# Two transformer layers on one core: the planner's passes, layer 0's queries through DRAM, and the first loads on two queues

## The chip, the cores and the metric

The kernel runs on one core of a Trainium2 chip. The metric is the device time of one execution in microseconds (us), given as the median over runs. A core has five engines with instruction streams of their own: TensorE (PE, with its weight loads shown apart as PEld), VectorE (DVE), ScalarE (ACT), GpSimd (POOL) and SyncE (SP, which issues most DMAs here). They meet through semaphores.

## The reference

Two layers over four batches of 256 rows of 512 numbers, all in float32, with a context of 1601 rows for each batch. Cut to what is computed:

```python
# layer 0: latent cross attention (16 heads, latent width 32) and an int4 FFN
C_q = ln(x) @ Wq_d                       # 512 -> 64
C_kv = ctx @ Wkv_d                       # 512 -> 32, shared by all heads
q0 = (C_q @ W_qk).reshape(b, n, 16, 32)
attn = softmax(q0 @ C_kv.T / sqrt(32))
x = x + attn @ (C_kv @ Wv_u)             # per head
x = x + ln(x) @ dequantize(weight_q, scale, zero_point).T + bias
# layer 1: grouped-query attention (16 heads, 4 KV heads, width 96), keys from [ctx, ln(x)]
q, k, v = ln(x) @ Wq.T, concat(ctx, ln(x)) @ Wk.T, concat(ctx, ln(x)) @ Wv.T
x = x + softmax(q @ k.T / sqrt(96)) @ v @ Wo.T
# layer 1: FFN with gated low-rank experts
H = ln(x) @ W.T + b;  z = ln(x) @ A
gate = f(H[:, 1::2, :8] / max|H|, (z[:, 1::2] @ LiMEs.T) / max|.|)  # softmax, soft top 2, over all batches
x = x + H + ((z * (gate @ LiMEs)) @ Bmat) * scaling
```

The two maxima in the gate go over all four batches, so the last part of the program waits for the last batch.

## The kernel before

**Stages.** A string, LINE (L1533 on), gives the order of the attention heads: 16 of layer 0 for batch 0, then, three times, a mix of layer 1's 16 heads of one batch with layer 0's 16 heads of the next, and then 16 heads of layer 1 for batch 3. Between a batch's two kinds of heads stand the layer-0 FFN (tiles f0) and layer 1's queries, keys and values.

**Order.** All work between the first loads and the gate is a set of tasks with hand-written costs, buffers and dependencies. `Plan.order` (L63 to L134) places them in one pass: of all tasks that are ready it takes the one with the earliest start, then the lowest `prio` (the place of its head in LINE plus an offset such as AT_SCORES). The result is the program order of every engine, the DMA queue on SP included; each engine then works strictly in that order. A task that needs a buffer can't be placed until the ring of its tag has a free one: 8 buffers for scores in SBUF ("S"), two for scores in PSUM ("s"), two for the stage tag "p" (normalised rows, parts of w0, and the query rows of layer 1 on their way to DRAM), two for layer 0's queries ("q0"), one for the transposed context ("ctxT", 3.3 MB).

**One head.** PE makes transposed scores in tiles of 32 rows, four side by side (L1306 in layer 0, L1382 in layer 1). ACT copies them to SBUF (L1162), DVE takes maxima over the key tiles (L1180 to L1188), PE turns the result (L1211), DVE reduces it (L1215), PE spreads it (L1224), DVE copies it (mB, L1232) and subtracts it from the scores (L1241), ACT takes the exponential (L1250), and PE multiplies with the values (L1333 in layer 0 with tiles of 64 columns, L1407 in layer 1 with full tiles). Between the heads PE makes K (L795) and V (L737) of the next layer-1 stage from the context.

**Layer 0's queries** (L643 to L669). For a pair of heads two matmuls of 64x128 by 64x256 (L649) give the queries of the pair, each copied four times over the partitions, since the score tiles use four row groups. The weights w_qk are loaded four times for that (L209 on, eight DMAs). ACT copies 512 columns to the q0 buffer (L658). Layer 1's queries go another way: PE, ACT into a stage of tag "p", a DMA to DRAM (q_rows), and DMAs back into the four row groups.

**FFN weights of layer 0** (make_w0, L477 on). Loads of the integers, zero points and scales, then DVE and POOL work, into w0T (L510 is POOL's).

**Start.** All loads are on SP: x, wq_d, w_qk, wkv_d, context, values' weights, keys' weights. POOL makes the identity matrix.

**End.** end_layer1 (L1526) normalises, calls l1_gate (z, g and d by PE, L1017 to L1081), and the FFN (tiles f, L532). After the plan come the gate's steps by DVE, POOL and ACT (L1659 to L1709), its transpose (wts_tp, L1716), the mix (L1721) and the output (L1740).

Of the kernel before, what the change touches and what calls it, by code (L numbers as in the profile page):

```python
# [62 lines left out]
class Plan:  # L63

    LAG = {"PE": 0.2, "ACT": 0.1, "DVE": 0.07, "POOL": 0.15, "SP": 0.05, "INIT": 0.0}
# [4 lines left out]
    def task(self, eng, us, what, deps=(), prio=0.0, new=(), uses=(), lag=0.0):  # L70

        t = Task(eng, us, what, [d for d in deps if d is not None], prio, new, len(self.tasks))
        t.lag = lag
        for b in (*new, *uses):
            b.users.append(t)
        self.tasks.append(t)
        return t

    def order(self, busy):

        free, ready, rings, done = {}, {}, {}, []
        for t in self.tasks:
            t.wait = len(t.deps)
            for d in t.deps:
                d.next.append(t)
            free.setdefault(t.eng, busy.get(t.eng, 0.0))
            ready.setdefault(t.eng, [])
            if not t.wait:
                t.at = 0.0
                ready[t.eng].append(t)  # L90

        def buffers(t):
            at, more = 0.0, {}
            for b in t.new:
                ring = rings.setdefault(b.tag, [])
                n = len(ring) + more.get(b.tag, 0)
                more[b.tag] = more.get(b.tag, 0) + 1
                if n >= b.bufs:
                    for u in ring[n - b.bufs].users:
                        if u.end is None:  # L100
                            return None
                        at = max(at, u.end + self.LAG[u.eng])
            return at

        while len(done) < len(self.tasks):
            best = None
            for eng, tasks in ready.items():
                for t in tasks:
                    at = buffers(t) if t.new else 0.0
                    if at is None:  # L110
                        continue
                    key = (max(free[eng], t.at, at), t.prio, t.key)
                    if best is None or key < best[0]:
                        best = (key, t)
            if best is None:
                stuck = [t for tasks in ready.values() for t in tasks]
                raise ValueError(f"no task can start: {[(t.eng, [b.tag for b in t.new], t.prio) for t in stuck]}")
            t = best[1]
            ready[t.eng].remove(t)
            t.start = best[0][0]  # L120
            free[t.eng] = t.start + t.us
            t.end = t.start + t.us + t.lag
            for b in t.new:
                rings[b.tag].append(b)
            for n in t.next:
                n.wait -= 1
                if not n.wait:
                    n.at = max(
                        d.end + (0.0 if d.eng == n.eng and not d.lag else self.LAG[d.eng])
                        for d in n.deps  # L130
                    )
                    ready[n.eng].append(n)
            done.append(t)
        return done  # L134


@with_exitstack
def xattn_ffn_x2_kernel(
# [47 lines left out]
    ident = const.tile([P, P], F32, name="ident")  # L186
    make_identity(nc, ident)
    neg_half = const.tile([P, NQ], F32, name="neg_half")
    nc.gpsimd.memset(neg_half, -0.5)

    xs = {}
    held = tc.dram_tile([NT * P, D], F32, name="held")

    for t in range(NQ):
        xs[t] = work.tile([P, D], F32, tag="x", bufs=2 * NQ, name=f"x_{t}")
        nc.sync.dma_start(out=xs[t], in_=x[t * P : (t + 1) * P, :])

    def load_ctx(b):  # L200
        t = big.tile([P, NC, S], F32, tag="ctxT", name=f"ctxT_{b}")
        src = ctxT[b].rearrange("(c p) s -> p c s", p=P)
        for a, w in ((0, 512), (512, 512), (1024, S - 1024)):
            nc.sync.dma_start(out=t[:, :, a : a + w], in_=src[:, :, a : a + w])
        return t

    wq_d_sb = const.tile([P, NC, LQ], F32, name="wq_d_sb")
    nc.sync.dma_start(out=wq_d_sb, in_=wq_d.rearrange("(c p) n -> p c n", p=P))


    w_qk_sb = const.tile([P, H0 // 2, 4, L0], F32, name="w_qk_sb")
    for r in range(4):
        for k in range(2):
            nc.sync.dma_start(
                out=w_qk_sb[k * LQ : (k + 1) * LQ, :, r, :],
                in_=w_qk.rearrange("q (k h l) -> k q h l", k=2, l=L0)[k],
            )
    wkv_d_sb = const.tile([P, NC, L0], F32, name="wkv_d_sb")
    nc.sync.dma_start(out=wkv_d_sb, in_=wkv_d.rearrange("(c p) n -> p c n", p=P))
    first_ctx = load_ctx(0)  # L220
# [3 lines left out]
    for r in (0, 64):  # L224
        nc.sync.dma_start(
# [8 lines left out]

    KV_ORDER = [3, 0, 1, 2]
    wvT_sb = const.tile([P, NC, KV * HD], F32, name="wvT_sb")
    for c in range(NC):
        src = wvT[c * P : (c + 1) * P, :]
        nc.sync.dma_start(out=wvT_sb[:, c, :HD], in_=src[:, 3 * HD :])
        nc.sync.dma_start(out=wvT_sb[:, c, HD:], in_=src[:, : 3 * HD])  # L240
# [48 lines left out]
    rsums = tc.dram_tile([B * KV, G * T], F32, name="rsums")  # L289
    q_rows = [  # L290
# [18 lines left out]
    def item(name, steps, evictions, deps, prio, uses=(), new=()):  # L309
# [5 lines left out]
        for us, what in steps:  # L315

            def run(what=what, first=last is None):
# [14 lines left out]
                [*uses] if first else [ps, *uses],  # L332
            )
# [214 lines left out]
    def l0_latents(b, deps, prio):  # L548
# [22 lines left out]
        def keep(ps):  # L571
# [11 lines left out]
            [cT],  # L583
        )
# [30 lines left out]
    def l0_query_latent(b, xnT, deps, prio):  # L615
        cqT = Buf("cqT", 1)


        def step(ps, c):
            for r in range(2):  # L620
                nc.tensor.matmul(
                    ps[r * LQ : (r + 1) * LQ, :T],
                    lhsT=wq_d_sb[:, c, :],
                    rhs=xnT.tile[:, c, :],
                    start=(c == 0),
                    stop=(c == NC - 1),
                )

        def keep(ps):
            nc.scalar.copy(cqT.tile, ps[:, :T])  # L630
# [9 lines left out]
            [(cqT, [P, T])],  # L640
        )

    def l0_query(b, pair, prio):  # L643
        q0, cqT = Buf("q0", 2), st8[b]["cqT"]

        def step(ps, j):
            h = 2 * pair + j
            half = slice(h // 8 * LQ, (h // 8 + 1) * LQ)
            nc.tensor.matmul(  # L649
                ps[:, j * T : (j + 1) * T],  # L650
                lhsT=w_qk_sb[half, h % 8, :, :].rearrange("q r l -> q (r l)"),
                rhs=cqT.tile[half, :],
# [4 lines left out]
        def keep(ps):  # L657
            nc.scalar.copy(q0.tile.rearrange("p j t -> p (j t)"), ps)  # L658

        st8[b]["q0", pair] = q0  # L660
        st8[b]["q0_done", pair] = item(
            f"q0_ps_{b}_{pair}",
            chain(2, mm(T), step),
            [("ACT", cp(512), keep, (), ())],
# [3 lines left out]
            [(q0, [P, 2, T])],  # L668
        )  # L669

# [343 lines left out]
    def l1_gate(b, xnT, deps, w, prio):  # L1014
# [10 lines left out]
        def z_keep(ps):  # L1025
# [11 lines left out]
            [xnT],  # L1037
        )
# [71 lines left out]

    AT_SCORES = -3.0
    AT_COPY = -1.1
    AT_MAX = -1.4
    AT_TURN = -0.9
    AT_SPREAD = -0.5
    AT_SUB0 = -0.6
# [4 lines left out]
    AT_FIN = -2.7  # L1121

    class Head:
# [6 lines left out]
        def schedule(self):  # L1130
# [6 lines left out]
            for groups, units in self.score_units():  # L1137
                for k, (us, what) in enumerate(units):

                    def run(what=what, groups=groups, first=k == 0):  # L1140
# [12 lines left out]
                        self.score_uses() + ([ps[g] for g in groups] if k else []),  # L1153
                    )
# [98 lines left out]
            for g in range(4):  # L1253
                n = self.groups[g] * T
                t = task(
                    "DVE",
                    tt(n),
                    lambda g=g: subtract(g),
                    [t],
                    at + (AT_SUB0 if g < 2 else AT_SUB1),  # L1260
                    uses=[S4[g], mb],
                )
                weighed.append(
                    task(
                        "ACT",
                        cp(n) + 0.05,
                        lambda g=g: weights(g),
                        [t],
                        at + (AT_EXP0 if g < 2 else AT_EXP1),
                        uses=[S4[g]],  # L1270
                    )
                )

            for us, groups, deps, uses, what in self.product_units():
# [6 lines left out]
                    uses=[om, *(S4[g] for g in groups), *uses],  # L1281
                )
            self.finish(om, t)

    class Head0(Head):
        layer, groups, scale = 0, [4, 4, 3, 2], 1.0 / math.sqrt(L0)

# [68 lines left out]
    class Head1(Head):  # L1356
        layer, groups, scale = 1, [4, 4, 4, 3], 1.0 / math.sqrt(HD)

# [119 lines left out]
    def load_context(b, prio):  # L1478
# [5 lines left out]
        st8[b]["cT_done"] = [task("SP", 0.3, run, book.get("x", ()), prio, [cT], lag=kb(3300))]  # L1484

    def start_layer0(b, at, deps):
# [3 lines left out]
        l0_latents(b, st8[b]["cT_done"], at - 5)  # L1490

    def context_work(b, at, deps_v, deps_k):
# [3 lines left out]
        for i in range(3):  # L1496
            ctx_keys(b, i, done + deps_k, at[0] - 4 + 0.2 * i)
        for half in range(2):
            new_values(b, half, at[2 * half] - 4)
            for t in range(NK0):  # L1500
                prio = at[0] - 3 + 1.5 * half + 0.05 * t
                values(b, half, t, cT, ctx_at[t], done + deps_v, prio)
# [59 lines left out]
    st8[0]["cT_done"] = [task("INIT", 0.0, have_ctx, new=[cT], lag=24.0)]  # L1562
    start_layer0(0, 0, ready(7.0))
    w0, w0_done = make_w0(st8[0]["cqT_done"])
    context_work(0, first1[0], ready(33.0), ready(40.0))
    for pair in range(2):
        l0_query(0, pair, -4)
    matrix, matrix_done = w0, w0_done
    for i, (layer, b, h) in enumerate(line):
        where = at[2 * b + layer]  # L1570
        if layer == 0:
            if h % 2 == 0 and h >= 4:
                l0_query(b, h // 2, i - 3)
            elif h == 0 and b:
                for pair in range(2):
                    l0_query(b, pair, i - 4)
# [76 lines left out]
    with tc.manual_schedule(engines=engines):  # L1653
        for t in plan.order({"SP": 40.0}):
# [137 lines left out]
```

## Time and profile before

| | |
|---|---|
| runs | 2025.68, 2028.62, 2031.17 us; median 2028.62 |
| profiled execution | 2031.49 us, span 2029.7 us |
| mean granted clock of TensorE | 0.979 |
| PE, DVE, ACT, POOL busy | 1960.7, 1379.7, 1172.5, 130.6 us |
| first PE instruction, first scores of layer 0 | 13.06, 30.49 us |
| last product of batch 0's layer 0 copied (L1350) | 230.8 us |
| first f0, first layer-1 scores | 252.46, 282.49 us |
| last FFN (f, L532), gate's weights (wts) | 1995.60 to 2005.1, 2007.47 us |
| DMA traffic | 99.01 MB, mean 49 GB/s |

Times inside the execution are microseconds from the start of the span. "Idle before" of a group is the time that its engine stood still before it, with what ended it. A group is named by line, engine, operation, and output and input tiles; a chain gives the work that ended last, in order of time; a window gives busy times of every engine in a stretch.

### The profile page before, as it was taken

The numbers are of one execution on the slowest core, as the hardware profiler recorded it, in microseconds if no ns is written. First come the engines' busy times: TensorE is split into PE (matmuls) and PEld (weight loads), VectorE is DVE, ScalarE is ACT, GpSimd is POOL, SyncE is SP. The second block draws the span as 40 slices with busy tenths as digits, with TensorE's granted clock in tenths as the row PEclk, the third lists the DMA queues.
The fourth block names the chain that finished last, engine by engine and source line by source line (L and its number), as shares of the span: only waits on it lengthen the run. The fifth ranks groups of instructions, "written<-read, shape, count | busy, mean of one in ns | idle before, by whom it ended". The sixth has DMA issues, their size and how long they took to land.

```text
span 2029.7 us, 35881 instructions
## 1 busy us (share of the span) xinstructions
PE 1960.7 (97%) x14873; PEld 1356.1 (67%) x14873; DVE 1379.7 (68%) x2077; ACT 1172.5 (58%) x1776; POOL 130.6 (6%) x171
## 2 busy tenths in 40 slices
PE   6999889999999999999999999999999999999977
PEld 4555667666766686766666777766666668677753
DVE  3876447877787635777778745587888764577653
ACT  3777336666666534666767644466676654465540
POOL 0100200000000100000000200000000010000000
PEclk9999899999999999999999999999999999999996
DMA  6000331110000024121000130512100002211221
GB/s 171 27 1 1 103 104 37 48 40 25 24 17 22 22 63 155 49 53 40 24 17 9 22 83 22 157 48 55 33 16 17 22 21 63 82 50 46 61 59 41
DMA packets 125574, 99.01 MB, mean 49 GB/s; under 512 B 71043, under 2 KB 103971, under 8 KB 125028
## 3 DMA queue, kind: packets, MB, share of 16 engines
q1 hardware_dynamic: 125412, 96.73, 17.2%
q8 instruction: 117, 1.92, 0.4%
q14 instruction: 45, 0.37, 0.1%
HBM read 85.51 MB, written 11.17 MB: 48 GB/s over the span
## 4 chain that ended last, share of the span: by engine, by line
PE 91%; ACT 3%; DVE 2%; DMA 2%; issue 1%; POOL 1%; SPq 0%; ACTq 0%; POOLq 0%; DVEq 0%
PE o L1407 20%; PE s L1382 18%; PE o L1333 10%; PE v_ps L737 8%; PE k_ps_c L795 7%; PE s L1306 7%; PE wo_ps L996 4%; PE q_ps L886 4%; PE f L532 3%; PE o L1211 2%; PE o L1224 2%; PE q_ps L649 1%; PE vu_ps L678 1%; PE k_ps_x L795 1%; ACT S L1250 1%
## 5 line engine op out<-in xcount | busy, mean ns | idle before, releaser
L1162 ACT COPY S<-s 128x1024 f32<-128x1024 f32 (+2 forms) x512 | 449.2, 906 | 374.6 <-PE s L1382 149.3
L1183 DVE TENSOR_TENSOR mx<-mx,S 128x512 f32<-128x512 f32 (+1 forms) x704 | 463.7, 659 | 127.5 <-ACT S L1162 101.1
L1241 DVE TENSOR_TENSOR S<-S,mB 128x1024 f32<-128x1024 f32 (+2 forms) x512 | 532.2, 1097 | 4.4
L1250 ACT ACTIVATE S<-S 128x1024 f32<-128x1024 f32 (+2 forms) x512 | 464.1, 946 | 97.6 <-DVE S L1241 91.1
L1407 PE MATMUL o<-S,v 128*97 128x256 f32 x1920 | 459.7, 383 | 2.1 <-ACT S L1250 2.1
L1407 PEld LDWEIGHTS o<-S,v 128*97 128x97 f32 x1920 | 302.5, 164 | 106.1 <-issue 20.7
L1382 PE MATMUL s<-q,kT_k_ps_c 32*128 32x256 f32 x4320 | 281.0, 386 | 2.2 <-ACT S L1162 1.7
L1382 PEld LDWEIGHTS s<-q,kT_k_ps_c 32*128 32x128 f32 x4320 | 227.7, 186 | 53.3 <-issue 20.8
L1333 PE MATMUL o<-S,ckv 128*64 128x256 f32 x1664 | 229.7, 393 | 4.2 <-ACT S L1250 3.9
L1333 PEld LDWEIGHTS o<-S,ckv 128*64 128x64 f32 x1664 | 115.8, 138 | 103.4 <-ACT S L1250 27.3
L795 PE MATMUL k_ps_c<-ctxT,wk_sb 128*128 128x384 f32 (+1 forms) x480 | 163.6, 462 | 0.2
L737 PE MATMUL v_ps<-wvT_sb,ctxT 128*128 128x192 f32 x832 | 163.2, 337 | 0.0
L1306 PE MATMUL s<-q_q_ps,ckvT 32*128 32x256 f32 x1664 | 150.3, 409 | 3.8 <-ACT S L1162 3.8
L737 PEld LDWEIGHTS v_ps<-wvT_sb,ctxT 128*128 128x128 f32 x832 | 134.8, 192 | 26.1 <-issue 21.7
L1215 DVE TENSOR_REDUCE m<-o 128x2 f32<-128x256 f32 x128 | 54.0, 422 | 130.6 <-PE o L1211 130.6
L1180 DVE TENSOR_TENSOR mx<-S 128x512 f32<-128x512 f32 x128 | 90.8, 709 | 58.5 <-ACT S L1162 58.4
L1306 PEld LDWEIGHTS s<-q_q_ps,ckvT 32*128 32x128 f32 x1664 | 91.8, 185 | 57.1 <-issue 33.0
L795 PEld LDWEIGHTS k_ps_c<-ctxT,wk_sb 128*128 128x128 f32 x480 | 77.3, 189 | 56.3 <-issue 25.5
L996 PE MATMUL wo_ps<-wo,oT 128*128 128x512 f32 x192 | 96.0, 624 | 10.3 <-POOL oT L983 10.3
L886 PE MATMUL q_ps<-xnT_xn_tp_a,wq 128*128 128x256 f32 x384 | 99.9, 392 | 1.4 <-issue 0.8
L805 ACT COPY kT_k_ps_c<-k_ps_c 32x384 f32<-32x384 f32 (+1 forms) x180 | 76.8, 426 | 33.4 <-PE k_ps_c L795 31.2
L1382 PE MATMUL s<-q,kTlast_k_ps_c 32*128 32x256 f32 x1440 | 93.2, 385 | 0.0
(136 smaller groups left out, 1411.6 us busy)
## 6 DMA issues: line engine op xcount, KB each, us to landing
q<-q_rows SPq DMA_DIRECT2D x192, 96.0 KB
wq<-in_wqT SPq DMA_DIRECT2D x48, 192.0 KB
wo<-in_woT SPq DMA_DIRECT2D x16, 576.0 KB
ctxT<-in_ctxT SPq DMA_DIRECT2D x8, 1024.0 KB
q_rows<-p_q_ps SPq DMA_DIRECT2D x48, 128.0 KB
q<-q_rows SPq DMA_DIRECT2D x192, 32.0 KB
ctxT<-in_ctxT SPq DMA_DIRECT2D x4, 1154.0 KB
rb<-rsums SPq DMA_DIRECT2D x16, 288.0 KB
```

The lines of the kernel that those rows point to most:

```text
L737: nc.tensor.matmul(ps[:, : 2 * HD], lhsT=src.tile[:, c, a : a + P], rhs=wvT_sb[:, c, half * 2 * HD : (half + 1) * 2 * HD], start=(c == 0), ...
L795: nc.tensor.matmul(out, lhsT=wk_sb[:, c, i, :], rhs=rhs, start=(c == 0), stop=(c == NC - 1),)
L886: nc.tensor.matmul(ps[:, :T], lhsT=wq.tile[:, c, :], rhs=xnT.tile[:, c, :], start=(c == 0), stop=(c == NC - 1),)
L996: nc.tensor.matmul(ps, lhsT=oT.tile[:, i, q * P : (q + 1) * P], rhs=wo.tile[:, i, :], start=(i == 0), stop=(i == G - 2),)
L1162: nc.scalar.copy(S4[g].tile[:, :n, :], self.scored(ps[g].tile, g))
L1183: nc.vector.tensor_tensor(mx.tile[:, :w, :], mx.tile[:, :w, :], t[:, a : a + w, :], ALU.max)
L1241: nc.vector.tensor_tensor(s[:, :n, :], s[:, :n, :], mb.tile[:, None, :].to_broadcast([P, n, T]), ALU.subtract,)
L1250: nc.scalar.activation(s[:, :n, :], s[:, :n, :], AF.Exp, scale=self.scale)
L1306: nc.tensor.matmul(pss[2 * step + r // 2][:, 2 * (r % 2) + s % 2, :], lhsT=st8[self.b]["ckvT"].tile[part, s, :], rhs=qr[part, self.h % 2, ...
L1333: nc.tensor.matmul(po[64 * par : 64 * par + 64, :], lhsT=s["ckv"].tile[:, t, :, :].rearrange("p o l -> p (o l)"), rhs=self.S[g].tile[:, i, :],
L1382: nc.tensor.matmul(pss[2 * step + r // 2][:, 2 * (r % 2) + slot % 2, :], lhsT=s["kT", self.kv].tile[part, c, slot, :], rhs=s["q1", self.kv ...
L1407: nc.tensor.matmul(po[:VW, :], lhsT=s["v", j // 2].tile[:, t, j % 2, :], rhs=self.S[g].tile[:, i, :], start=(k == 0), stop=(k == NK1 - 1),)
```

## The change

It has three parts.

1. **Planner.** Every task of PE has a form (full, 32 rows, 64 columns, 32 columns, 64 rows). `forward` is the old pass with new constants; a change of form costs SWITCH and adds HOLD to the priority of a task. `backward` goes through the finished order from its end and sets each task's priority to how late it has to end. `order` alternates the two, nine forward passes in all, and keeps the order whose own end is the earliest. The offsets AT_ of the first pass and the due times of the first loads are new too.
2. **Layer 0's queries.** One matmul of 64x128 by 64x256 for four heads, one copy into a stage of tag "p", one DMA to DRAM (q0_rows), and then four DMAs for each pair back into the four row groups. w_qk is loaded once.
3. **Start.** x, wq_d, wkv_d, w_qk and wv_h are loaded by ACT's queue, the context, wv and wk by SP's. The identity is made by DVE from a counted row and a column that is loaded, and POOL's first power is issued at once.

The diff, cut (lines of SELF and OVERLAP are the engines' own gaps; `backward` is left out):

```diff
-    LAG = {"PE": 0.2, "ACT": 0.1, "DVE": 0.07, "POOL": 0.15, "SP": 0.05, "INIT": 0.0}
+
+    LAG = {"PE": 0.22, "ACT": 0.05, "DVE": 0.05, "POOL": 0.1, "SP": 0.05, "INIT": 0.0}
+    SELF = {"ACT": 0.012, "DVE": 0.034}
+    OVERLAP = {"ACT": 0.1, "DVE": 0.084}
+
+
+    SWITCH = 0.2
+    HOLD = 2.0
...
+                    stays = eng != "PE" or t.form == form
+                    key = (
+                        max(free[eng], t.at, at),
+                        t.prio + (0.0 if stays else self.HOLD),
+                        t.key,
+                    )
...
+            if t.eng == "PE" and t.form != form:
+                t.start += self.SWITCH
+            free[t.eng] = t.start + t.us - self.OVERLAP.get(t.eng, 0.0)
...
+    ROUNDS = 8
+
+    def order(self, busy):
+        for t in self.tasks:
+            for d in t.deps:
+                d.next.append(t)
+        best = None
+        for i in range(self.ROUNDS + 1):
+            done = self.forward(busy)
+            end = max(t.end for t in done)
+            if best is None or end < best[0]:
+                best = (end, done)
+            self.backward(done)
+        return best[1]
...
-    ident = const.tile([P, P], F32, name="ident")
-    make_identity(nc, ident)
+
     neg_half = const.tile([P, NQ], F32, name="neg_half")
     nc.gpsimd.memset(neg_half, -0.5)
-
-
-
+    first_power = small.tile([P, NQ], F32, tag="power", bufs=1, name="first_power")
+    nc.gpsimd.memset(first_power, 1.0)
+    nc.gpsimd.tensor_tensor(first_power, first_power, neg_half, ALU.pow)
     xs = {}
-    held = tc.dram_tile([NT * P, D], F32, name="held")
-
     for t in range(NQ):
         xs[t] = work.tile([P, D], F32, tag="x", bufs=2 * NQ, name=f"x_{t}")
-        nc.sync.dma_start(out=xs[t], in_=x[t * P : (t + 1) * P, :])
-
-    def load_ctx(b):
+        nc.scalar.dma_start(out=xs[t], in_=x[t * P : (t + 1) * P, :])
+
+    count = ptile("count")[:, :P]
+    nc.vector.memset(count[:, 0:1], 0.0)
+    for k in (1, 2, 4, 8, 16, 32, 64):
+        nc.vector.tensor_scalar(count[:, k : 2 * k], count[:, :k], float(k), None, ALU.add)
+    number = small.tile([P, 1], F32, tag="number", bufs=1, name="number")
+    nc.scalar.dma_start(out=number, in_=count[0:1, :])
+    ident = const.tile([P, P], F32, name="ident")
+    nc.vector.tensor_scalar(ident, count, number, None, ALU.is_equal)
+    wq_d_sb = const.tile([P, NC, LQ], F32, name="wq_d_sb")
+    nc.scalar.dma_start(out=wq_d_sb, in_=wq_d.rearrange("(c p) n -> p c n", p=P))
+    wkv_d_sb = const.tile([P, NC, L0], F32, name="wkv_d_sb")
+    nc.scalar.dma_start(out=wkv_d_sb, in_=wkv_d.rearrange("(c p) n -> p c n", p=P))
+    w_qk_sb = const.tile([LQ, H0 * L0], F32, name="w_qk_sb")
+    nc.scalar.dma_start(out=w_qk_sb, in_=w_qk)
...
+    first_ctx = load_ctx(0, load_wv)
...
         def step(ps, c):
-            for r in range(2):
-                nc.tensor.matmul(
-                    ps[r * LQ : (r + 1) * LQ, :T],
-                    lhsT=wq_d_sb[:, c, :],
-                    rhs=xnT.tile[:, c, :],
-                    start=(c == 0),
-                    stop=(c == NC - 1),
-                )
+            nc.tensor.matmul(
+                ps[:LQ, :T],
+                lhsT=wq_d_sb[:, c, :],
+                rhs=xnT.tile[:, c, :],
+                start=(c == 0),
+                stop=(c == NC - 1),
+            )
         def keep(ps):
-            nc.scalar.copy(cqT.tile, ps[:, :T])
+            nc.scalar.copy(cqT.tile, ps[:LQ, :T])
         st8[b]["cqT"] = cqT
         st8[b]["cqT_done"] = item(
@@ -637,36 +718,58 @@
             deps,
             prio,
             [xnT],
-            [(cqT, [P, T])],
+            [(cqT, [LQ, T])],
+            "64 columns",
         )
-    def l0_query(b, pair, prio):
-        q0, cqT = Buf("q0", 2), st8[b]["cqT"]
-
-        def step(ps, j):
-            h = 2 * pair + j
-            half = slice(h // 8 * LQ, (h // 8 + 1) * LQ)
+    def l0_query(b, quad, prio):
+
+        stage, cqT, far = Buf("p", 2), st8[b]["cqT"], q0_rows[b * H0 // 4 + quad]
+
+        def step(ps, _):
             nc.tensor.matmul(
-                ps[:, j * T : (j + 1) * T],
-                lhsT=w_qk_sb[half, h % 8, :, :].rearrange("q r l -> q (r l)"),
-                rhs=cqT.tile[half, :],
+                ps[:, :T],
+                lhsT=w_qk_sb[:, quad * P : (quad + 1) * P],
+                rhs=cqT.tile,
                 start=True,
                 stop=True,
             )
         def keep(ps):
-            nc.scalar.copy(q0.tile.rearrange("p j t -> p (j t)"), ps)
-
-        st8[b]["q0", pair] = q0
-        st8[b]["q0_done", pair] = item(
-            f"q0_ps_{b}_{pair}",
-            chain(2, mm(T), step),
-            [("ACT", cp(512), keep, (), ())],
+            nc.scalar.copy(stage.tile[:, :T], ps[:, :T])
+
+        def away():
+            nc.sync.dma_start(out=far, in_=stage.tile[:, :T])
+
+        t = item(
+            f"q0_ps_{b}_{quad}",
+            chain(1, mm(T), step),
+            [("ACT", cp(T), keep, (), ())],
             st8[b]["cqT_done"],
             prio,
             [cqT],
-            [(q0, [P, 2, T])],
+            [(stage, [P, 512])],
+            "64 rows",
         )
+        st8[b]["q0_away", quad] = [task("SP", 0.4, away, t, prio, uses=[stage], lag=2.5)]
+
+    def l0_query_pair(b, pair, prio):
+
+        q0, far = Buf("q0", 2), q0_rows[b * H0 // 4 + pair // 2]
+
+        def load():
+            t = make(q0, [P, 2, T], f"q0_{b}_{pair}")
+            a = pair % 2 * 2 * L0
+            for r in range(4):
+                nc.sync.dma_start(
+                    out=t[r * L0 : (r + 1) * L0],
+                    in_=far[a : a + 2 * L0].rearrange("(j l) t -> l j t", l=L0),
+                )
+
+        st8[b]["q0", pair] = q0
+        st8[b]["q0_done", pair] = [
+            task("SP", 1.6, load, st8[b]["q0_away", pair // 2], prio, [q0], lag=3.0)
+        ]
...
+    AT_COPY = -1.3
...
     def start_layer0(b, at, deps):
 
         xnT, done, _ = layernorm(b, "a0", "xnT", at - 5)
         l0_query_latent(b, xnT, done + deps, at - 5)
-        l0_latents(b, st8[b]["cT_done"], at - 5)
+        for quad in range(H0 // 4):
+            l0_query(b, quad, at - 4.5 + quad)
+        l0_latents(b, st8[b]["cT_done"][-1], at - 5)
...
+    st8[0]["cT_done"] = [[t, *ready(us)] for us in (8.0, 13.0, 16.0)]
+    start_layer0(0, 0, ready(5.0))
     w0, w0_done = make_w0(st8[0]["cqT_done"])
-    context_work(0, first1[0], ready(33.0), ready(40.0))
+    context_work(0, first1[0], ready(11.0), ready(21.0))
     for pair in range(2):
-        l0_query(0, pair, -4)
...
-        for t in plan.order({"SP": 40.0}):
+        for t in plan.order({"SP": 14.0}):
```

## The prediction

> **What bounds the kernel now.** I read the page's busy shares and chain first, then the windows by stage, then the chain of waits at the three places that the change touches: the start, the end of batch 0's layer 0, and the end of the program.
>
> ```profile
> PE 1960.7 (97%) x14873; PEld 1356.1 (67%) x14873; DVE 1379.7 (68%) x2077; ACT 1172.5 (58%) x1776; POOL 130.6 (6%) x171
> PE 91%; ACT 3%; DVE 2%; DMA 2%; issue 1%; POOL 1%; SPq 0%; ACTq 0%; POOLq 0%; DVEq 0%
> ```
>
> TensorE sets the time over most of the span: 91% of the chain is PE. So PE work that is removed counts in full, unless a stage is set by something else. The windows say where (time, then PE, PEld, DVE, ACT, POOL busy, clock):
>
> ```profile
> 50.00:100.00 50.00, 48.07 (x324) 28.62 (x324) 42.77 (x68) 38.69 (x60) 8.75 (x9) 1.00 0.09 28
> 100.00:150.00 50.00, 48.50 (x320) 28.26 (x320) 39.68 (x61) 38.52 (x60) 2.02 (x4) 0.97 0.00 1
> 240.00:290.00 50.00, 40.32 (x300) 30.64 (x303) 13.59 (x29) 9.43 (x25) 8.43 (x9) 0.84 0.36 97
> 1000.00:1200.00 200.00, 199.05 (x1473) 137.11 (x1470) 147.19 (x222) 131.10 (x204) 16.50 (x17) 0.99 0.08 22
> 1960.00:2030.00 70.00, 46.71 (x105) 21.95 (x103) 20.65 (x50) 4.19 (x9) 3.08 (x4) 0.67 0.14 48
> ```
>
> In the first two, batch 0's layer-0 heads, PE is full only because K and V work of layer 1 is mixed in, and VectorE is 80 to 86% busy: a head of layer 0 alone would be VectorE's. The next and the last are stages of waits, with PE at 81 and 67% and a lower clock.
>
> ```profile
> 227.58 0.38 SPq L204
> 229.16 10.12 DMA w_AluOpType.subtract<-in_zeroT
> 239.35 0.74 POOL w0T L510
> 252.46 6.88 PE f L532 x16
> ```
>
> After the last head of layer 0 (230.8) a small load, issued behind the 3.3 MB context load, takes 10.12 us; the FFN of layer 0 waits for it.
>
> ```profile
> 1988.77 3.59 PE z_ps L1017 x8
> 1995.04 0.56 PE d_ps L1081 x2
> 1995.60 6.09 PE f L532 x8
> 2007.47 0.20 DVE wts L1709
> 2007.81 0.46 PE wts_tp L1716
> ```
>
> At the end, z and d come before f, so the gate's chain (from d's end, 1995.6, to wts, 2007.67: 12.1 us) runs beside the last FFN (1995.6 to 2005.1).
>
> The sum is made against the profiled execution, 2031.49 us (span 2029.7, 1.8 around it). It lies 2.9 above the median, 2028.62. About 6 us, 0.3%, is what can be told from no change.
>
> **Queries of layer 0: PE and ACT work.** L649 runs 64 program matmuls of 256 columns, each in two passes (128 in the trace). Warm passes start 216 ns apart, so one costs 0.432 us. 16 remain: 48 x 0.432 = **-20.7 us** of PE. ACT's 32 copies of 588 ns become 16 of about 0.37 (the 256-column copy at L1350): -12.6 us, off the path, since ACT is 58% busy.
>
> **Form changes.** The new order has 775 changes between tile forms of matmuls, the old 855. A step that follows a change starts 309 ns after the last one instead of 216 (full to 32 rows), 256 instead of 162 (to 192 columns), so 0.09 to 0.1 us: 80 x 0.097 = **-7.8 us** in bounds 7.2 to 8.8. The Trainium skill, "TensorEngine Tiling (Array Packing)", says that changing the tiling mode drains the TensorE; it gives no price there. The planner's SWITCH of 0.2 would make it -16; the trace's steps say half of that, and the sum keeps -7.8.
>
> PE work in all: **-28 us**; of it 19 lies behind the first layer-1 score, 8.6 before.
>
> **Start.** The first PE instruction (13.06) hangs on POOL: 7.75 us of "issue" end at 9.24, then memsets, then the normalisation's power at 11.74 and DVE at 12.46. The loads are not in that chain. The 7.75 precede the first POOL custom work, and an early power (first_power) doesn't remove a wait that any such instruction would meet. The second queue for x therefore gains nothing, bounds -3 to +1; I take +0.5. The Trainium skill's "Trainium Kernel Development and Optimization" page says that queues of several engines share the same 16 DMA engines and save only issue time; this start shows no wait for issue time to be saved.
>
> The first queries now go to DRAM and back. The same path for layer 1 shows 2.96 us from the away's issue to the load's, then four loads issued in 1.86. From cq (19.6) with three V tiles ahead (3.9), the matmul and copy (1.0), 2.96, 1.86 and some 3 of landing: first scores at about 33.5, against 30.49.
>
> **Batch 0's heads, the deciding part.** The queries of quads 1 to 3 (heads 4 to 15) need a stage buffer of tag "p", of which there are two. In the new order the normalised rows of batch 1 hold both. PE's order is therefore heads 0 to 3; then, in one block, all that is left of batch 0's context work; then batch 1's transposes, q0 quads 1 to 3, cq of batch 1; and only then head 4's scores. The block: 20 V tiles x 8 passes x 162 ns = 26.0; 5 K chunks x 8 x 323 = 12.9; 2 narrow ones x 8 x 109 = 1.7; with transposes, q0 and cq (1.6 + 1.3 + 1.7) **45 us** in which VectorE has almost nothing to do. Before, this work was the filler between heads.
>
> The away for quad 1 stands on SP right behind batch 1's context load, which the block's end releases. The nearest row is the 10.12 us above; the other bound is the free path, 2.96. With the loads behind it, head 4's scores come 8 to 16 us after the block; I take 12, since the queue's order is that of the 10.12. Behind the away on SP stand the other q0 transfers and w0's scale load (L477), which has over 100 us until f0; PE alone waits.
>
> Heads 4 to 15 then run without filler. PE needs some 6.3 us for one, VectorE 9.4:
>
> ```profile
> L1183 DVE TENSOR_TENSOR mx<-mx,S 128x512 f32<-128x512 f32 x56 | 39.5, 705 | 11.2 <-ACT S L1162 8.9
> L1241 DVE TENSOR_TENSOR S<-S,mB 128x1024 f32<-128x1024 f32 x30 | 35.8, 1233 | 0.5
> L1241 DVE TENSOR_TENSOR S<-S,mB 128x768 f32<-128x768 f32 x15 | 14.3, 950 | 0.0
> L1241 DVE TENSOR_TENSOR S<-S,mB 128x512 f32<-128x512 f32 x15 | 10.5, 700 | 0.0
> ```
>
> That is 5 x 0.70 + 0.49 + 0.43 for the maxima, 0.42 each for reduce and mB, 2 x 1.23 + 0.95 + 0.70 for the subtractions: 9.4 per head, 113 for twelve. The max, transpose, reduce, spread and subtract chain crosses engines, so I take 122 to 125 (bounds 113 and 145, the old period of 12.1 each).
>
> Old: head 3's product ends near 85, head 15's at 230.8, f0 at 252.5. New: 85.5 + 45 + 12 + 124 = **267**. The weight chain (L477 on) is then long finished, so the 10-us load no longer matters, and f0 follows after 9 instead of 21.7: **276**. The first layer-1 score moves from 282.4 to 306: **+24 us** (bounds 0 and +42), with this stage's share of the PE saving already in it.
>
> **Middle.** From there PE work is 19 us shorter. Other stalls there (127 us to the end of the program) may move: VectorE's share grows as PE shrinks, 160.4 of 200 at 1400 to 1600, and SP gains 124 DMAs of away and load. Both-sided, -10 to +15; I take 0.
>
> **End.** The new order runs g, f1, then z, d. The planner's end leaves out the gate chain after its schedule. From xnT (1988.63): g 2.4, f1 9.5, z 1.8 to 3.6, copies and d 1.0, chain 12.1 less the two residual additions of 0.64 (now beside it): wts at 2014 to 2017, against 2007.67. **+8 us**, bounds +6 and +9. Cover gone: f1 hid that chain.
>
> Sum: +24 - 19 + 8 = +13, with the start inside the +24: 2044.5 against 2031.49, **2042** against the median.
>
> **Rivals.** (a) *Faster*: the block is harmless. VectorE's floor holds (113), the round trip hides (wait 1), so head 15 ends at 245 and f0 starts at 254: stage 0 costs 1 or 2, and -19 + 8 + 2 = -9, or -19 if 10 us of other stalls go: 2010 to 2020. For it: VectorE's busy share of 86% with 9.4 us per head. Against it: PE then waits for ACT and VectorE in every head, with only two score buffers. (b) *The parts cancel*: heads at 9.4, wait 10; stage 0 costs +11 and the total is 0, near 2029. (c) *Much slower*: the heads without filler take 11 us (chain-bound, and at a half clock as at 157.3 to 164.1, after PE idles) and the next stages' stalls grow by 10: 2065. It decides once a head's period passes 10.5. (d) *The change doesn't do what it says*: form changes fall by 80 only; were the price zero, 8 us more, 2050, inside the forecast's own range, 2032 to 2060.
>
> **How the numbers follow.** Forecast 0.57, (a) 0.22, (b) 0.12, (c) 0.09; (d) is in the forecast. Hence faster 0.22, same 0.12, slower 0.66. The range takes in the forecast, (b), the upper half of (a) and the lower part of (c): 2012 to 2066.
>
> **What the changed profile would show.** First scores near 33.5, PE's first instruction still at 13; a stretch of PE near 100% and VectorE under 30% at about 87 to 130; a PE idle stretch of 8 to 16 us behind it, released by the load of q0; then VectorE over 90% busy and PE near 65% until about 267; f0 near 276; 12 us without PE between d and wts_tp. The forecast is wrong if head 4's scores start before 135, if the twelve heads take under 115 us, or if the stages after the first layer-1 score shorten by over 30.

## The result, and the profile after

The changed kernel takes 2048.26 us (median of 4 runs, 2044.78 to 2049.47); the kernel before, run beside it, 2027.88. The ratio is 1.0092 with a 95% interval of 1.0073 to 1.0112: slower by 0.9%, 20.4 us of medians. The two profiled executions, 2031.49 and 2048.03 us, differ by 16.5; the account below goes by these.

The page, busy shares and chain:

```profile
PE 1938.2 (95%) x14745; PEld 1348.3 (66%) x14745; DVE 1371.1 (67%) x2086; ACT 1156.6 (57%) x1760; POOL 117.4 (6%) x171
PE 79%; DVE 8%; ACT 6%; issue 4%; DMA 3%; POOL 1%; SPq 0%; POOLq 0%; DVEq 0%; ACTq 0%
```

PE's work did shrink, by 22.5 us of busy time; but it now carries 79% of the chain instead of 91%. The chain runs through VectorE, ScalarE and DMA for what PE gave up. The windows (time, then PE, PEld, DVE, ACT, POOL busy, clock) say where:

```profile
90.00:130.00 40.00, 37.57 (x197) 31.06 (x196) 0.47 (x2) 16.47 (x45) 0.85 (x3) 1.00 0.00 0
150.00:200.00 50.00, 41.46 (x257) 22.32 (x258) 43.11 (x64) 30.88 (x43) 7.32 (x7) 0.81 0.23 73
1000.00:1200.00 200.00, 198.00 (x1519) 133.64 (x1513) 153.26 (x229) 139.95 (x210) 13.31 (x17) 1.00 0.06 17
1960.00:2046.00 86.00, 57.25 (x155) 29.59 (x153) 29.61 (x63) 11.81 (x21) 4.02 (x5) 0.72 0.18 59
```

From 90 to 130 VectorE works 0.47 us of 40: that is the block of K and V work. From 150 to 200 the heads without filler follow: VectorE at 86%, PE at 83% of a slower clock. Between the two stands this stretch of the chain:

```profile
133.32 0.39 SPq L293
...
134.91 9.66 DMA q_rows<-p_q_ps
...
144.59 1.74 DMA q<-q_rows
146.32 0.04 issue
146.37 3.56 PE s L1400 x11
```

L293 is the context load of batch 1; the queries' way to DRAM, issued right behind it, takes 9.66 us, and head 4's scores start when they are back.

By stage, from the traces (start of the first, end of the last matmul named; us):

| | before | after | change in the stretch |
|---|---|---|---|
| first PE instruction | 13.1 | 16.0 | +2.9 |
| first scores of layer 0 | 30.4 | 35.8 | +2.5 |
| head 3's product ends | 87.3 | 89.7 | -3.0 |
| head 4's scores start | 65.3 | 146.4 | |
| head 15's product ends | 230.7 | 276.9 | +43.8 |
| f0 of batch 0 starts | 252.3 | 284.5 | -14.0 |
| first layer-1 score | 282.4 | 313.3 | -1.3 |
| last product of layer 1 ends | 1965.1 | 1976.1 | -19.9 |
| wts_tp | 2007.8 | 2024.6 | +5.8 |
| last output matmul ends | 2025.9 | 2042.6 | -0.1 |

So the first stage loses 31 us, the long middle wins 20, the end loses 6. Each column is one execution; four runs below that share one order there (own_stage and three that change only its ends) differ by up to 8 us in the middle, so a few us can't be read from it.

### The profile page after: what moved, and what is told of

Same layout as the page of the kernel before. It is cut to its first block, busy times and chain, and to the rows that moved or that the text cites. A ratio compares the mean times of both kernels' runs of the same rounds, so it can differ in the third digit from the quotient of the medians.

```text
span 2046.2 us, 35954 instructions
## 1 busy us (share of the span) xinstructions
PE 1938.2 (95%) x14745; PEld 1348.3 (66%) x14745; DVE 1371.1 (67%) x2086; ACT 1156.6 (57%) x1760; POOL 117.4 (6%) x171
## 3 DMA queue, kind: packets, MB, share of 16 engines
q1 hardware_dynamic: 131236, 105.84, 18.3%
## 4 chain that ended last, share of the span: by engine, by line
PE 79%; DVE 8%; ACT 6%; issue 4%; DMA 3%; POOL 1%; SPq 0%; POOLq 0%; DVEq 0%; ACTq 0%
PE o L1502 18%; PE s L1477 16%; PE o L1427 9%; PE v_ps L840 6%; PE k_ps_c L898 6%; PE s L1400 6%; PE q_ps L989 4%; DVE mx L1287 3%; PE wo_ps L1099 3%; DVE S L1345 2%; PE f L614 2%; ACT S L1266 2%; ACT S L1354 2%; PE o L1315 2%; PE o L1328 1%
## 5 line engine op out<-in xcount | busy, mean ns | idle before, releaser
L1354 ACT ACTIVATE S<-S 128x1024 f32<-128x1024 f32 (+2 forms) x512 | 481.7, 952 | 252.1 <-DVE S L1345 248.3
L1345 DVE TENSOR_TENSOR S<-S,mB 128x1024 f32<-128x1024 f32 (+2 forms) x512 | 552.5, 1109 | 2.7
L1477 PEld LDWEIGHTS s<-q,kT_k_ps_c 32*128 32x128 f32 x4320 | 227.3, 185 | 47.3 <-issue 19.9
L1427 PE MATMUL o<-S,ckv 128*64 128x256 f32 x1664 | 237.8, 397 | 20.4 <-ACT S L1354 20.3
L1400 PE MATMUL s<-q,ckvT 32*128 32x256 f32 x1664 | 157.9, 420 | 10.6 <-DMA q<-q_rows 8.0
L898 PE MATMUL k_ps_c<-ctxT,wk_sb 128*128 128x384 f32 (+1 forms) x480 | 156.8, 453 | 2.6 <-ACT xnT_xn_tp_f L517 1.1
L840 PE MATMUL v_ps<-wvT_sb,ctxT 128*128 128x192 f32 x832 | 153.0, 332 | 1.6 <-ACT v L849 1.6
L1400 PEld LDWEIGHTS s<-q,ckvT 32*128 32x128 f32 x1664 | 98.4, 190 | 64.2 <-issue 35.5
```

The lines of the kernel that those rows point to most:

```text
L840: nc.tensor.matmul(ps[:, : 2 * HD], lhsT=src.tile[:, c, a : a + P], rhs=wvT_sb[:, c, half * 2 * HD : (half + 1) * 2 * HD], start=(c == 0), ...
L898: nc.tensor.matmul(out, lhsT=wk_sb[:, c, i, :], rhs=rhs, start=(c == 0), stop=(c == NC - 1),)
L1345: nc.vector.tensor_tensor(s[:, :n, :], s[:, :n, :], mb.tile[:, None, :].to_broadcast([P, n, T]), ALU.subtract,)
L1354: nc.scalar.activation(s[:, :n, :], s[:, :n, :], AF.Exp, scale=self.scale)
L1400: nc.tensor.matmul(pss[2 * step + r // 2][:, 2 * (r % 2) + s % 2, :], lhsT=st8[self.b]["ckvT"].tile[part, s, :], rhs=qr[part, self.h % 2, ...
L1427: nc.tensor.matmul(po[64 * par : 64 * par + 64, :], lhsT=s["ckv"].tile[:, t, :, :].rearrange("p o l -> p (o l)"), rhs=self.S[g].tile[:, i, :],
```

## The experiments

All medians are from runs beside the kernel before on the same chip; ratios are to it. Its own median was 2027.5 to 2030.8 over these sessions, so medians of different sessions compare to some 3 us. The diffs are cut. "New planner" is the changed one, "old planner" the constants, offsets and single pass of before.

**own_stage: the block's cause.**

```diff
-        stage, cqT, far = Buf("p", 2), st8[b]["cqT"], q0_rows[b * H0 // 4 + quad]
+        stage, cqT, far = Buf("q0s", 2), st8[b]["cqT"], q0_rows[b * H0 // 4 + quad]
...
-            [(stage, [P, 512])],
+            [(stage, [P, T])],
```

> The stage of layer 0's queries gets a tag of its own (two buffers of 128x256), planned anew; all else as in the changed kernel. Theory (the tag 'p' that the queries share with the normalised rows made the 45-us block of context work, the wait and twelve heads without filler): the K and V work spreads over all 16 heads, first layer-1 score at 280 to 290 instead of 313, time 2010 to 2020. Rival (the loss lies in the way through DRAM or in the nine passes themselves): the first layer-1 score stays over 300 and the time stays at 2040 or more.

Measured: 2022.98 us, ratio 0.9972 (0.9955 to 0.9989); first layer-1 score at 287.4. The windows:

```profile
50.00:100.00 50.00, 47.79 (x357) 28.00 (x355) 44.23 (x70) 42.05 (x66) 1.50 (x2) 1.00 0.07 22
150.00:200.00 50.00, 48.85 (x347) 33.57 (x348) 40.02 (x62) 40.72 (x70) 4.14 (x6) 1.00 0.03 6
```

VectorE and PE are now busy side by side in both, at full clock. One buffer tag took 25 us off the median; in the traces 26 lie ahead of the first layer-1 score, and the middle (1660.5 us from there to the last product, against 1662.8) stayed. The theory stands for the place; the total is 3 us above its range.

**away_first: can the wait alone be taken away?**

```diff
+        steps = plan.order({"SP": 14.0})
+        late = st8[1]["cT_done"][0][0]
+        steps.remove(late)
+        steps.insert(steps.index(st8[0]["q0_done", 3][0]) + 1, late)
```

> The order of the changed kernel, with one move: on SP, batch 1's context load goes behind the DRAM round trip of the queries of heads 4 to 7. Theory: the 8.0 us wait before head 4 shrinks to 3 or less, and with it the half clock of 27 us behind it may go: 5 to 15 us less than the changed kernel, 2033 to 2043. Rival (the wait is covered, VectorE's heads set the end anyway): 2046 to 2049.

Measured: 2046.22 us, ratio 1.0093 (1.0061 to 1.0125), where the changed kernel has 1.0092. Head 4's scores start at 138.2 instead of 146.4, but head 8's at 183.7, as in the changed kernel (183.4). The waits between 137 and 160:

```profile
ACT p_q_ps L739 <- DMA q_rows<-p_q_ps: 10.9, 1, 10.9
PE s L1400 <- ACT S L1266: 11.4, 2, 11.2
```

ScalarE's copy of batch 1's first query needs a "p" buffer whose own way to DRAM still stands behind the context load; ScalarE works in order, so head 4's score copies wait behind that copy, and PE behind them. The wait changed its name, and nothing was won.

**old_queries and old_planner: one half of the change at a time.** old_queries puts the functions of before (L615 to L669) and their eight w_qk loads back, on ACT's queue:

```diff
+            [(q0, [P, 2, T])],
...
-        st8[b]["q0_away", quad] = [task("SP", 0.4, away, t, prio, uses=[stage], lag=2.5)]
...
-            l0_query(b, quad, at - 4.5 + quad)
```

old_planner puts back the constants, the offsets and the single pass:

```diff
-    SWITCH = 0.2
-    HOLD = 2.0
+    SWITCH = 0.0
+    HOLD = 0.0
...
-    ROUNDS = 8
+    ROUNDS = 0
...
-    AT_COPY = -1.3
+    AT_COPY = -1.1
```

> New planner and new start, but layer 0's queries as before (two matmuls a pair, no DRAM). Theory: no block either, but 20.7 us more PE work than with the new queries, so 2030 to 2040, some 20 above own_stage. Rival (the DRAM path costs more than the matmuls it saves): at or below own_stage.

> New queries (stage of tag 'p') and new start, but the planner's constants, offsets and single pass as before. In its order the block of context work (42.8 us) stands before head 8 instead of head 4. Theory: the block comes with the shared tag, whatever the planner; eight heads without filler instead of twelve: 2035 to 2050, first layer-1 score at 300 to 310. Rival (the nine passes make the block's cost): 2025 or less.

Measured: 2043.55 us, ratio 1.0078 (1.0050 to 1.0105), and 2073.88 us, ratio 1.0230 (1.0197 to 1.0263). old_queries lies 20.6 above own_stage, as its theory said, though its range was missed by 4. That this is the 20.7 of PE work isn't shown: in the traces its first layer-1 score comes 9.7 us sooner than own_stage's (277.7 against 287.4), and its middle takes 32 longer. old_planner has the block too, and is far above its range: the shared tag does it under either planner. Against own_old_planner below, whose tag is its own, its first layer-1 score comes 34 us later (323.7 against 290.1); under the new planner the tag cost 26. So eight heads without filler did not cost less than twelve. Its middle takes 25 us more than the changed kernel's (1687.9 against 1662.8); own_old_planner's takes 18 more.

**own_old_planner and own_one_pass: what the nine passes are worth.** The first is own_stage with old_planner's edit, the second own_stage with one line of it:

```diff
-    ROUNDS = 8
+    ROUNDS = 0
```

> The missing one of four: the planner's constants, offsets and single pass as before, with the new queries in a stage of their own, new start. Theory (the block gone, but the old single pass leaves PE with the stalls that old_planner had behind the first layer-1 score, 116 us against 76 with the nine passes): 2035 to 2050. Rival (the new queries' 28 us of PE work count in full under either planner): 2000 to 2010.

> own_stage with one forward pass instead of nine (the new costs and offsets stay). Form changes 747 instead of 770 in its order, so PE work is 2 us less. Theory (the passes from the end place DVE's and ACT's work so that PE stalls less; with the old planner and the new queries the stretch from the first layer-1 score to the last product had 116 us of stalls, with the nine passes 76): 15 to 35 us slower than own_stage, 2038 to 2058. Rival (the form costs and offsets did it): within 5 us of own_stage.

Measured: 2029.24 us, ratio 0.9999 (0.9981 to 1.0017), and 2060.61 us, ratio 1.0143 (1.0118 to 1.0168). The first is 6 under its range and the second 3 over it; both rivals are far off. With the old planner the new queries are worth nothing, although they take the same matmuls off PE. The windows from the first layer-1 score to the last product show where it goes (before, the change, own_old_planner, own_one_pass, own_stage):

```profile
282.42:1965.06 1682.64, 1670.01 (x13105) 1174.05 (x13104) 1193.32 (x1757) 1012.37 (x1502) 97.69 (x113) 1.00 0.17 47
313.27:1976.10 1662.83, 1642.11 (x13030) 1168.01 (x13030) 1183.23 (x1756) 998.64 (x1489) 86.56 (x113) 1.00 0.19 51
290.09:1971.26 1681.17, 1651.50 (x13017) 1165.80 (x13016) 1188.74 (x1757) 1003.20 (x1488) 94.84 (x113) 0.99 0.18 51
290.36:1992.17 1701.81, 1652.81 (x13017) 1164.92 (x13016) 1181.42 (x1757) 997.59 (x1488) 89.03 (x113) 0.99 0.18 50
287.41:1947.95 1660.54, 1637.59 (x13030) 1165.13 (x13030) 1181.81 (x1756) 999.11 (x1489) 88.44 (x113) 1.00 0.19 51
```

In own_old_planner PE is busy 18.5 us less than before, but stands still 29.7 us instead of 12.6: the gain went into gaps. In own_one_pass it stands still 49.0 us, in own_stage 23.0. So the nine passes are worth 38 us of median with the new costs and offsets; but these alone, in one pass, are some 30 worse than the old ones, and the new planner as a whole wins some 6 over the old. What makes DVE's and ACT's work fall better was not shown. The table of medians:

| | queries as before | new, tag "p" | new, own tag |
|---|---|---|---|
| old planner | 2028 (before) | 2073.9 | 2029.2 |
| new planner | 2043.6 | 2048.3 (the change) | 2023.0 |

The parts don't add up: under the new planner the new queries in their own stage win 20.6, under the old one nothing (the start differs too in that row, which own_start_old below finds to be worth nothing). Why the new planner is 16 slower than the old with the queries of before stays open; its loss lies behind the first layer-1 score (1692.6 us to the last product, against 1682.6, and 5 more to the end), and no run here takes that apart.

**own_switch_tenth: the price of a form change.**

```diff
-    SWITCH = 0.2
+    SWITCH = 0.1
```

> own_stage with the planner's price of a form change at 0.1 us, the trace's, instead of 0.2. Its order has 791 form changes instead of 770, by the prediction's step 2 us more PE work. Theory (a form change costs 0.1 us and no more, the rest is the order's own luck): 2018 to 2032. Rival (form changes cost 0.2 us or more): the work between the first layer-1 score and the end rises by over 4 us.

Measured: 2012.40 us, ratio 0.9914 (0.9886 to 0.9943), 10.6 below own_stage and below the theory's range. From the first layer-1 score to the last product it takes 1655.9 us, against own_stage's 1660.5, with 21 form changes more in the program. The rival falls, since the stretch did not rise by 4 (tenth_tail's below, of the same order, is 1655.7); its fall is within what one order shows from run to run. The step between matmuls at a change is the same in the changed kernel as before: 309 ns from full to 32 rows at 256 columns, against 216. That the lower price is what made the order better, and not the order's luck, isn't shown by one order.

**own_z_first and own_wo_early: the end.** Each is own_stage's order with one move. own_z_first's lines come first: the gate's tasks of the last batch go before its FFN's. own_wo_early's move the third group's output projection on PE before the last head's product.

```diff
+        first, then = book["end"]
+        moved = [t for t in steps if t in first]
+        steps = [t for t in steps if t not in first]
+        where = steps.index(next(t for t in steps if t in then))
+        steps[where:where] = moved
...
+        where = steps.index(book["product"])
+        late = [t for t in steps[where:] if t in book["out"]]
+        steps = [t for t in steps if t not in late]
+        where = steps.index(book["product"])
+        steps[where:where] = late
```

> own_stage with one move at the end of the program: z and d of the last batch go before the last FFN's matmuls, as before the change. By the prediction's term (the FFN hid a chain of 12.1 us) the stretch from the last transposes to wts_tp falls by 8, from 23.7 to about 16. By the trace of the changed kernel, where the chain from d to wts_tp takes only 6.3 us once nothing stands in between, the old order was itself held up by the residual add that DVE has to do after the FFN, and the stretch falls by 2, to the 21.5 of before.

> own_stage with one move on PE: the last two steps of the output projection of the third head group go before the product of the last head instead of behind it, so that its weights' buffer comes free, and the last 768 KB of output weights are loaded, some 7 us earlier. Theory (that load, issued 1 us ahead of the row sums' way through DRAM, slows it: 4.7 and 3.8 us instead of 1.6 and 2.5): row sums' DMAs at their times of before, last product to last transposes 25.4 -> 21 or 22, time 3 to 4 less. Rival (their time is their own): unchanged.

Measured: 2022.52 us, ratio 0.9961 (0.9939 to 0.9983), and 2022.56 us, ratio 0.9962 (0.9948 to 0.9976), neither to be told from own_stage by the median. The stretches tell: last transposes to wts_tp 21.3 us instead of 23.7 in the first, as the second reading said, not 16; last product to last transposes 20.5 instead of 25.4 in the second, with the row sums' transfers back at their times:

```profile
1960.22 1.60 DMA rsums<-sums
...
1963.18 2.40 DMA rb<-rsums
```

**own_start_old: the start.** own_stage's order, with x, the small weights and wv_h on SP and the identity on POOL.

```diff
-    nc.gpsimd.tensor_tensor(first_power, first_power, neg_half, ALU.pow)
+    make_identity(nc, ident)
...
-        nc.scalar.dma_start(out=xs[t], in_=x[t * P : (t + 1) * P, :])
+        nc.sync.dma_start(out=xs[t], in_=x[t * P : (t + 1) * P, :])
...
-    nc.scalar.dma_start(out=w_qk_sb, in_=w_qk)
+    nc.sync.dma_start(out=w_qk_sb, in_=w_qk)
```

> own_stage's order with the first loads and the identity as before the change (all loads on SP, x first, identity on POOL; w_qk still loaded once). Theory (the loads on two queues, 249 instead of 211 GB/s in the first 30 us, slow what POOL's first library instruction waits for, 10.4 instead of 7.8 us): PE's first instruction at 13 instead of 16.4, 2 to 4 us less in all. Rival (POOL's wait comes from the power being first): first instruction stays at 16; or the later loads hold PE up and the gain is lost before the first scores.

Measured: 2025.12 us, no clear difference from own_stage. The chain:

```profile
1.49 7.44 issue
...
26.60 7.89 DMA q<-q_rows
```

PE's first instruction comes at 12.8 instead of 16.4, so the number of the theory's first half held, though the loads and POOL's first instruction were changed together and its reason isn't shown; the first scores gain only 1.6 (34.5), since the queries' loads then wait 7.89 us among the other loads, and nothing is left at the first layer-1 score (287.1 against 287.4).

**own_tail and tenth_tail: the moves together.** own_tail is own_stage with both moves at the end, tenth_tail is own_switch_tenth with them (the diffs above).

> own_stage with both moves at the end of the program: z and d before the last FFN, and the output projection's last two steps of the third group before the last product. Theory, from the traces of the single moves: last transposes to wts_tp 21.3 instead of 23.7, last product to last transposes 20.5 instead of 25.4 with 1.7 of it moved ahead of the product: 5 to 6 us less than own_stage, 2017, and faster than both kernels. Rival (the moves only shift the waits): 2022 as own_stage.

> own_switch_tenth (queries' stage of its own, form change priced at 0.1) with own_tail's two moves at the end of the program. Theory: the 5 us that the moves gave over own_stage come again, since they touch only the last 70 us: 2007, with last transposes to wts_tp at 18 to 19 instead of 22.2. Rival (half of it, because own_switch_tenth's last product already ends with less of the output projection behind it): 2010.

Measured: 2017.75 us, ratio 0.9941 (0.9918 to 0.9964), and 2006.31 us, ratio 0.9896 (0.9866 to 0.9926). In both, wts_tp comes 18.3 us after the last transposes begin, 3 sooner than z's move alone gave; by the medians the two moves give 5 or 6 us, by the ratios 6 and 4, as expected. tenth_tail beats the kernel before by 1% and the changed one by 2%.

## Why the prediction was right, and where its steps were off

**The block** was forecast at 45 us from 85.5 to 130.5; head 3's product ended at 89.7 (before: 87.3, not "near 85") and the block's last matmul (cq of batch 1) at 138.4, 48.7 later. own_stage shows its cause to be the shared tag.

**The wait behind the context load** was taken as 12 in bounds of 8 to 16; it is 8.0 (138.4 to 146.4), the transfer itself 9.66 against the 10.12 of the row it was taken from. A half clock came with it, which the forecast left to rival (c):

```profile
138.40:146.40 8.00, 0.04 (x2) 0.03 (x1) 0.00 (x0) 0.63 (x2) 0.00 (x0) 0.63 0.81 297
146.40:167.80 21.40, 20.24 (x90) 12.28 (x92) 13.37 (x21) 9.75 (x15) 1.26 (x1) 0.50 0.33 99
```

The granted clock is at half from 140.5 to 167.8; in away_first, where PE waits 11.2 us, from 146.4 to 166.9, and in own_stage, without such a wait, not at all between 50 and 229. The Trainium skill, "TensorE: Matmul & The Clock Gate", Part 1, says that an idle window of about 3.4 us puts TensorE back at half clock; the 8.0 us wait agrees, though the drop stands only 2.1 us behind the last matmul. Why the clock stayed down for 21.4 us of work, in which the profile has PE busy for 20.24, is open, and so is what it cost.

**Heads 4 to 15** were forecast at 124 us and took 130.5. VectorE's price was right: it was busy 111.1 us of these, against 113. The last eight products ended 9.1 apart (204.2 to 276.9). The first four took 57.8 from the first score; at half clock for 21 us of it, but head 0, at full clock, also took 23.8 from its first score to its product's end, and head 4 took 26.4. How much was such filling and how much the clock isn't shown. PE was busy for 85% of the stretch, not "near 65%".

**The start** was a step that failed: its term of +0.5, with bounds of -3 to +1, measured +2.9. The terms for the first scores add up to 32.3 (32.8 with the 0.5), not 33.5; they came at 35.8.

```profile
1.38 10.38 issue
11.76 0.74 POOL first_power L262
...
15.98 1.97 PE xn_tp_a L509 x8
```

POOL's wait did stay, as said, but it grew from 7.75 to 10.38 us; own_start_old shows it at 7.44 with the old loads and identity. Whether the loads (249 GB/s in the first 30 us against 211) or the kind of POOL's first instructions makes it longer was not taken apart.

**The middle**: -19 forecast, -19.9 measured, and this closeness is partly luck. In the traces 72 of the passes that went (88 of L649, now 16 of L730) and 74 of the form changes (700, now 626) lie in this stretch; at the prediction's own prices that is 15.6 + 7.2 = 22.8, not 19, and the measured 19.9 can't tell the two apart. The price of a change held, since its step stayed at 309 ns against 216. PE stands still 20.7 us there instead of 12.6. That the stalls would neither grow nor shrink was a guess that nearly held for this order; own_old_planner shows that it need not: there the same saving bought nothing. (The SP DMAs that layer 0's queries add behind the first layer-1 score are 96, not 124.)

**The end**: +8 forecast, +5.8 measured, and for another reason. The gate's term failed: 12.1 us was not the chain's length. Before the change, DVE stood in it:

```profile
2001.71 0.69 DVE x L524
2002.51 0.18 DVE inv L1666
```

The residual add waits for the FFN, and the rest of the gate's chain stands behind it in DVE's order, so the FFN didn't hide the chain, it held it up. With nothing in between, the changed kernel needs 6.2 us from d's end (2018.35) to wts_tp. That term was worth 2.1 us (own_z_first: 2.4). The other 3.6 were in no step of the prediction; the row sums' way through DRAM, before and then after the change:

```profile
1967.72 1.60 DMA rsums<-sums
...
1970.68 2.48 DMA rb<-rsums
```

```profile
1978.80 4.71 DMA rsums<-sums
...
1984.87 3.79 DMA rb<-rsums
```

The last output weights were issued 0.95 us ahead of the row sums and shared the queue with them; own_wo_early brings 1.60 and 2.40 back. So the forecast's +8 came near the 5.8 by luck.

Sum: stage 0 +31 instead of +24, middle -20 instead of -19, end +6 instead of +8: 17 in the traces where 13 was said. In stage 0 the later head 3, the longer block and the heads add 14 us to the forecast, and the shorter wait and the quicker way to the first layer-1 score take 7 back.

**The rivals.** (a) failed on the block; with the block gone, own_stage comes within 3 us of its 2010 to 2020. (b) failed by 20. (c) gave the half clock rightly, but its instance was misread: ahead of 157.3 in the kernel before, PE was busy for 9.66 of 10.3 us. Its period of 10.5 was passed on average (10.9 for the twelve heads), but not by the last eight. (d) fell with the step of a form change: 80 fewer, at a price that stayed.

## What to carry to other kernels

A new user of a shared ring of buffers takes part in an order that was right for the old users: look at who holds the ring's buffers while the new one waits, and what the planner fills the gap with. Work that is taken off the bounding engine pays only if the schedule closes the gaps behind it: the same 20.7 us of matmuls were worth 21 under one planner and nothing under another. And before a chain's length is priced, take out of it the instructions that wait for something else on the same in-order engine.

## What the runs showed of the hardware that was not expected

POOL's first arithmetic instruction waited 7.75 and 7.44 us in the two kernels with the loads on one queue and the identity on POOL (before and own_start_old), 10.38 us in the changed kernel, which puts loads on two and the power first, and 9.8 to 11.5 us over all twelve kernels that do. A 4 KB transfer to DRAM took 4.71 us behind 768 KB on the same queue and 1.60 without it. The granted clock fell to half 2.1 us into a wait of PE of 8.0 us, and stayed there for 21.4 us behind the wait, of which the profile has PE busy for 20.24.
